# Semaphore increments without a waiter between the depthwise-convolution matmuls of a four-layer image network

## The chip, the core and the metric

The kernel runs on one core of one Trainium2 chip. The core has five engines with an instruction stream each: TensorE (matmuls; "PE" in the profile, its weight loads "PEld"), VectorE ("DVE"), ScalarE ("ACT"), GpSimd ("POOL") and SyncE ("SP", which here issues transfers). [...] an instruction may wait until a counter has a value, and may add one to a counter when it is done. The metric is the device time of one launch in microseconds.

## What is computed

The input `x` is 4 images of 48 channels, 256 by 256, in fp32. Four layers follow each other, each `x = x + layer(group_norm(x))`. Layers 1 and 2 are scans over rows and columns with a small convolution per step, and layer 0 resembles layer 3. The change is in layer 3:

```
def _L3_conv_ref(x, w_in, w_dw, fft_mask, w_out):
    ...
    y = jnp.einsum('oc,bchw->bohw', w_in, x)
    ...
    f = jnp.fft.rfft2(yp) * fft_mask[None]
    yp = jnp.fft.irfft2(f, s=(P, P))
    ...
    y = lax.conv_general_dilated(y, w_dw, window_strides=(1, 1), padding=((1, 1), (1, 1)), dimension_numbers=('NCHW', 'OIHW', 'NCHW'), feature_group_count=C2)
    x1, x2 = jnp.split(y, 2, axis=1)
    g = jax.nn.gelu(x1, approximate=False) * x2
    return jnp.einsum('oc,bchw->bohw', w_out, g)
```

48 channels are widened to 288, each 8 by 8 patch goes through a Fourier transform, is scaled and comes back, then every channel is convolved by itself with a 3 by 3 filter (the nine "taps"), the halves are gated, and 144 channels are narrowed to 48 again.

## The kernel before

Two images are worked on at once, in strips of 8 rows: 32 full strips and one tail strip of a single row for each pair of images, so 64 full strips and 2 tails in `layer3` (line 881 on). The transforms are matmuls too: `turned` (`pt`, L1006), `waves` (`pf`, L1021), `spectrum` and `spectrum_rest` (`pz`, L1040 and L1053), `pixels` and `pixels_rest` (`pp`, L1087 and L1106). They leave the strip's widened channels in SBUF tiles named `z_a0`, `z_a1` (two halves of the first 128 channels of one image), `z_b0`, `z_b1` (the other image) and `z_m` (what remains of both).

The 3 by 3 convolution is shared between two engines. VectorE computes the upper four rows of the `z_b` tiles by multiply-and-add (`begin`, L1183). Everything else goes to TensorE as matmuls with diagonal weights: a tap is the strip, shifted by the tap's offset, times a 32x32 diagonal matrix of filter values, added up in PSUM over nine taps. The array of 128x128 is used as 16 places of 32x32, four blocks of 32 channels by four groups of output partitions.

This work is cut into two "lanes". Lane 0 has channel blocks 0 and 1, lane 1 has blocks 2 and 3. A unit is one lane's nine taps for one tile: `taps` (L1117 to L1127; matmul at L1123) for `a0`, `a1` and `m`, and `lower_taps` (L1130 to L1144; matmul at L1139) for the lower rows of both `b` tiles. In both, a tap is eight matmuls of 32x512: in `taps` the row pair `j` runs from 0 to 3 and for each the two blocks of the lane; in `lower_taps` it is two halves, two row pairs and two blocks. In a tail strip `taps` has `j = 0` only, and `lower_taps` isn't called.

`together` (L1272) runs two units side by side: one tap of lane 0, one tap of lane 1, and so on nine times, with one of VectorE's multiply-adds issued now and then between them. A strip has seven units (three for each lane, and `m`, which goes to lane 0 in even strips and lane 1 in odd ones), so two strips make seven such pairs. Layer 3 is recorded under a hand-written schedule: TensorE, VectorE and ScalarE execute in the order in which the code issues.

When a unit is done its sums leave PSUM through `curve` (gelu on ScalarE, L1160) and `gate` (product on VectorE, L1166) or `lower_gate` (L1146). Between two pairs of units TensorE does transforms or the final narrowing (`mixed`, `po`, L1205 and L1215).

## Time and profile before

| | us |
|---|---|
| timed runs, median of 3 | 13250.55 (13233.93 to 13252.02) |
| profiled execution | 13259.28 |
| its span | 13257.5 |
| of it, reading the input and its statistics (0 to 230) | 230 |
| layer 0 (230 to 2790) | 2560 |
| layers 1 and 2, the scans (2790 to 8690) | 5900 |
| layer 3 (8690 to 13257) | 4567 |

The profile comes from one profiled execution. Its page gives each engine's busy time, the span in 40 slices, the DMA queues (one of them, "instruction", brings the engines' programs), the chain of work that ended last, and the costliest groups of instructions. A group is named by line, engine and operation, then the output and input tiles, the shape and a count. "Idle before" is how long the engine stood idle just ahead of that group, and behind the arrow stands what ended that wait; "issue" means that nothing that the profile shows was waited for. Semaphore instructions are not counted as busy. The ends of matmuls are modelled, and matmuls in different places of the array overlap, so a group's busy time is less than count times mean. The granted clock of TensorE over the whole execution was 0.966 of full speed.

### The profile page before, as it was taken

Reading aid. Unit: us, or ns where it says so; the run is one execution under the profiler, and the core shown is the slowest. Engines: PE = TensorE matmul, PEld = TensorE weight load, DVE = VectorE, ACT = ScalarE, POOL = GpSimd, SP = SyncE. Lnnn points to the kernel's source line nnn. Section 1 sums busy time; section 2 is a strip of 40 time slices with the busy share of each in tenths; the row PEclk is TensorE's granted clock in tenths of the full one; section 3 lists DMA queues with packets and bytes.
Section 4 is the critical chain, followed back from the end, with each engine's and each line's share of the span. In section 5 each row is a group of like instructions: output and inputs, shape, how many; then the busy total and the mean of one; then the engine's idle time right before and its main releaser. Section 6 shows DMA issues by size and latency. Waiting matters only on the chain.

```text
span 13257.5 us, 432328 instructions
## 1 busy us (share of the span) xinstructions
PE 12356.8 (93%) x203336; PEld 8155.9 (62%) x203336; DVE 7417.3 (56%) x10766; ACT 3602.9 (27%) x4043; POOL 1336.7 (10%) x977
## 2 busy tenths in 40 slices
PE   2999999998999899999998999989999999999999
PEld 1333333335777677767776777666666666666666
DVE  6777777773333334653333336556666666666666
ACT  1444444442223100002232000033333333333333
POOL 0011011010000002530000015400000000000000
PEclk9999999998999999999999999889999999999999
DMA  7222222225755876987657769711111111111110
GB/s 171 59 55 57 55 57 59 52 54 101 153 134 153 172 153 147 229 177 152 136 153 165 157 135 220 179 31 27 23 27 27 24 27 23 27 27 23 27 27 20
DMA packets 1170374, 1225.00 MB, mean 92 GB/s; under 512 B 1027669, under 2 KB 1031757, under 8 KB 1107725
## 3 DMA queue, kind: packets, MB, share of 16 engines
q1 hardware_dynamic: 1070476, 649.55, 25.6%
q0 software_dynamic: 87488, 445.55, 11.6%
q10 hardware_dynamic: 10624, 102.24, 4.4%
q8 instruction: 1592, 26.08, 0.9%
q14 instruction: 194, 1.58, 0.0%
HBM read 699.76 MB, written 497.42 MB: 90 GB/s over the span
## 4 chain that ended last, share of the span: by engine, by line
PE 88%; ACT 4%; issue 3%; DVE 3%; DMA 2%; SPq 0%; POOL 0%; DVEq 0%; ACTq 0%; POOLq 0%
PE acc L661 40%; PE pd L1123 12%; PE pd L308 9%; PE pd L1139 5%; PE pz L1040 4%; PE pp L1087 4%; PE po L1215 2%; PE ph L285 2%; PE pz L1053 2%; DMA gx<-in_x 1%; PE ph L277 1%; PE py L382 1%; PE po L452 1%; PE py L389 1%; PE po L1205 1%
## 5 line engine op out<-in xcount | busy, mean ns | idle before, releaser
L661 PE MATMUL acc<-line,w_down 96*96 96x256 f32 x12240 | 2692.9, 382 | 53.0 <-ACT line L731 31.8
L661 PEld LDWEIGHTS acc<-line,w_down 96*96 96x96 f32 x12240 | 2008.1, 164 | 730.1 <-DVE line L740 34.1
L1123 PE MATMUL pd<-z_a,diag 32*32 32x512 f32 x37152 | 1626.2, 599 | 57.8 <-issue 49.4
L308 PE MATMUL pd<-main,diag 32*32 32x512 f32 x36864 | 1427.2, 621 | 81.4 <-issue 77.3
L661 PE MATMUL acc<-line,w_right 96*96 96x256 f32 x6120 | 1341.0, 380 | 81.8 <-DVE line L811 59.8
L661 PE MATMUL acc<-line,w_left 96*96 96x256 f32 x6120 | 1362.9, 384 | 31.2 <-DVE line L852 31.2
L1183 DVE SCALAR_TENSOR_TENSOR acc<-z_b,wd,acc 128x1024 f32<-128x1024 f32 (+1 forms) x1056 | 1326.5, 1259 | 34.4 <-ACT acc L1178 7.1
L345 DVE SCALAR_TENSOR_TENSOR acc<-rest,wd,acc 128x1024 f32<-128x1024 f32 x1024 | 1257.8, 1292 | 126.9 <-ACT acc L339 126.6
L1123 PEld LDWEIGHTS pd<-z_a,diag 32*32 32x32 f32 x37152 | 890.6, 103 | 604.0 <-issue 232.9
L661 PEld LDWEIGHTS acc<-line,w_right 96*96 96x96 f32 x6120 | 1000.1, 164 | 412.6 <-DVE line L811 61.1
L661 PEld LDWEIGHTS acc<-line,w_left 96*96 96x96 f32 x6120 | 1007.9, 165 | 377.5 <-DVE line L852 47.1
L308 PEld LDWEIGHTS pd<-main,diag 32*32 32x32 f32 x36864 | 505.2, 105 | 798.1 <-issue 684.4
L1139 PE MATMUL pd<-z_b,diag 32*32 32x512 f32 x18432 | 973.7, 642 | 0.5 <-ACT z_b L999 0.5
L740 DVE TENSOR_TENSOR line<-acc,in 96x256 f32<-96x256 f32 x1020 | 428.9, 421 | 961.6 <-PE acc L661 948.7
L814 DVE SCALAR_TENSOR_TENSOR line<-acc,b_right,in 96x256 f32<-96x256 f32 x1020 | 489.4, 480 | 836.4 <-PE acc L661 836.4
L775 DVE SCALAR_TENSOR_TENSOR line<-acc,b_down,in 96x256 f32<-96x256 f32 x992 | 475.9, 480 | 811.5 <-PE acc L661 810.6
L120 ACT ACTIVATE nrm<-nrm 96x2 f32<-96x2 f32 (+2 forms) x5 | 1.0, 204 | 2989.4 <-DVE nrm L119 2989.4
L852 DVE SCALAR_TENSOR_TENSOR line<-acc,b_left,in 96x256 f32<-96x256 f32 x992 | 475.8, 480 | 564.2 <-PE acc L661 564.2
L862 POOL TENSOR_TENSOR blk<-blk,line 96x1024 f32<-96x1024 f32 x248 | 705.2, 2873 | 644.3 <-DVE line L852 644.3
L1043 DVE TENSOR_TENSOR z<-pz,mask 128x1024 f32<-128x1024 f32 x512 | 601.2, 1219 | 276.2 <-PE pz L1040 273.7
L782 ACT COPY blk<-line 96x1024 f32<-96x1024 f32 (+2 forms) x264 | 480.0, 1891 | 978.0 <-DVE line L775 816.0
L1087 PEld LDWEIGHTS pp<-c_inv,z 64*64 64x64 f32 x32768 | 515.9, 135 | 228.8 <-issue 204.6
(167 smaller groups left out, 13065.8 us busy)
## 6 DMA issues: line engine op xcount, KB each, us to landing
blk<-x ACTq DMA_DIRECT2D x64, 1536.0 KB, 19.3
in<-x SPq DMA_DIRECT2D x248, 384.0 KB, 11.0
dn<-line POOLq DMA_DIRECT2D x124, 768.0 KB, 9.6
rt<-line POOLq DMA_DIRECT2D x124, 768.0 KB, 9.6
in<-rt SPq DMA_DIRECT2D x124, 768.0 KB, 12.6
in<-dn SPq DMA_DIRECT2D x120, 768.0 KB, 5.8
in<-up SPq DMA_DIRECT2D x240, 384.0 KB, 9.3
up<-blk POOLq DMA_DIRECT2D x56, 1536.0 KB, 14.3
```

The lines of the kernel that those rows point to most:

```text
L308: nc.tensor.matmul(pd[32 * j : 32 * j + 32, i], diag[s, t, :], z[s, R2 * j + t // 3 : R2 * j + t // 3 + R2, t % 3 : t % 3 + W], start=(t = ...
L345: nc.vector.scalar_tensor_tensor(to, at(t, r), wd[:, 1, t : t + 1], to, ALU.mult, ALU.add)
L661: self.nc.tensor.matmul(acc, w[:, t, :], carry[:, :, t : t + m], start=(t == 0), stop=(t == 2))
L782: nc.scalar.copy(blk[:, :, e, lo:hi, k // 2 : k // 2 + RH], inner(ln[:, e::2])[..., lo:hi].rearrange("p h i w -> p i w h"),)
L814: nc.vector.scalar_tensor_tensor(blocks(inner(line)), blocks(acc), br, new, ALU.add, ALU.add)
L862: (nc.vector if w0 == 0 else nc.gpsimd).tensor_tensor(part, part, inner(ln[:, f::2])[..., lo:hi].rearrange("p w i h -> p i h w"), ALU.add)
L1040: nc.tensor.matmul(pz[:, b, q, :], xf[s, q0 + q, :], wi[s, NM * k : NM * k + NM], start=True, stop=True)
L1043: nc.vector.tensor_tensor(zs[k][:, q0 : q0 + 4].rearrange("p q b c -> p b q c"), pz, mask[:, :, :, NM * k : NM * k + NM].to_broadcast([128 ...
L1087: nc.tensor.matmul(pp[64 * c : 64 * c + 64, l, q, :], z[f, q0 + q, b, 64 * c : 64 * c + 64], self.inv1[f, :], start=True, stop=True,)
L1123: nc.tensor.matmul(pd[32 * j : 32 * j + 32, i, 0:n, :], diag[s, 2 if g == "m" else half, t, :], zt[g][s, R2 * j + t // 3 : R2 * j + t // 3 ...
L1139: nc.tensor.matmul(pd[to, i], diag[s, half, t, :], zt[f"b{half}"][s, R2 * j + t // 3 : R2 * j + t // 3 + R2, t % 3 : t % 3 + W], start=(t ...
L1183: nc.vector.scalar_tensor_tensor(acc, at(t), wd[:, half, t : t + 1], acc, ALU.mult, ALU.add)
```

## The change

A semaphore `pace` is allocated once, and in both tap functions an instruction that adds one to it is put into TensorE's stream: in `taps` behind every odd row pair `j`, in `lower_taps` behind each half. Either way it stands behind four matmuls of one lane. No instruction waits for `pace`, and nothing else differs.

```
+            pace = tc.alloc_semaphore("pace")
+
             def taps(step, g, half, blocks, pd):
                 for t in range(9):
                     for j in range(1 if tail(step) else 4):
...
                                 zt[g][s, R2 * j + t // 3 : R2 * j + t // 3 + n, t % 3 : t % 3 + W],
                                 start=(t == 0), stop=(t == 8),
                             )
+                        if j % 2:
+                            nc.tensor.sem_inc(pace)
                     yield True
 
             def lower_taps(step, blocks, pd):
...
                                     zt[f"b{half}"][s, R2 * j + t // 3 : R2 * j + t // 3 + R2, t % 3 : t % 3 + W],
                                     start=(t == 0), stop=(t == 8),
                                 )
+                        nc.tensor.sem_inc(pace)
                     yield True
```

In the built program each of these is one instruction of its own on TensorE, of the kind that the profile calls EVENT_SEMAPHORE.

More of the change, by code (lines that the diff above doesn't have):

```diff
@@ L1113, in pixels_rest @@
                         nc.scalar.copy(to[:, j, l], pp[64 * j : 64 * j + 64, l].rearrange("p q (h w) -> p q h w", w=8))
+            pace = tc.alloc_semaphore("pace")
             def taps(step, g, half, blocks, pd):
@@ L1127, in taps @@
                             )
+                        if j % 2:
+                            nc.tensor.sem_inc(pace)
                     yield True
@@ L1143, in lower_taps @@
                                 )
+                        nc.tensor.sem_inc(pace)
                     yield True
```

## The prediction

> **What bounds the kernel now.** I read the first lines of the page, then the chain of waits, then layer 3's stage alone, then one pair of tap units in the timeline.

> ```profile
> span 13257.5 us, 432328 instructions
> PE 12356.8 (93%) x203336; PEld 8155.9 (62%) x203336; DVE 7417.3 (56%) x10766; ACT 3602.9 (27%) x4043; POOL 1336.7 (10%) x977
> PE 88%; ACT 4%; issue 3%; DVE 3%; DMA 2%; SPq 0%; POOL 0%; DVEq 0%; ACTq 0%; POOLq 0%
> ...
> PE acc L661 40%; PE pd L1123 12%; PE pd L308 9%; PE pd L1139 5%; PE pz L1040 4%; PE pp L1087 4%; PE po L1215 2%; PE ph L285 2%; PE pz L1053 2%; DMA gx<-in_x 1%; PE ph L277 1%; PE py L382 1%; PE po L452 1%; PE py L389 1%; PE po L1205 1%
> q8 instruction: 1592, 26.08, 0.9%
> ```

> TensorE carries 88% of the chain, and the lines that the change touches carry 12% + 5% of it: 17% of 13257.5 us, 2254 us. Whatever the change adds to TensorE there lengthens the run; nothing else stands in front of it.

> ```profile
> 8690.00:13257.00 4567.00, 4376.90 (x127017) 3056.65 (x127014) 2934.61 (x3068) 1589.31 (x2325) 5.69 (x15) 0.97 0.12 25
> ```

> This is layer 3 alone (TensorE's matmuls, its loads, VectorE, ScalarE, GpSimd; then the granted clock): TensorE is busy for 4377 of 4567 us and VectorE for 2935, so no other engine is near. What TensorE waits for there is, by the view of waits, "issue" for 163.7 us (the six such rows added, 167 stalls) and everything else for 20 us.

> Now the taps themselves. Two views of one pair of units, both lanes on `z_a`:

> ```profile
> 11042.34 0.56 PEld L1123 LDWEIGHTS pd<-z_a,diag 32*32 32x32 f32 x33
> 11042.35 9.75 PE L1123 MATMUL pd<-z_a,diag 32*32 32x512 f32 x288
> ...
> 11043.23 0.55 PEld L1123 LDWEIGHTS pd<-z_a,diag 32*32 32x32 f32 x32 [0.33 <-issue]
> ...
> 11044.09 7.09 PEld L1123 LDWEIGHTS pd<-z_a,diag 32*32 32x32 f32 x223 [0.31 <-issue]
> ...
> 11051.80 1.94 ACT L1160 ACTIVATE gl<-pd 128x1024 f32<-128x1024 f32 x2 [7.24 <-PE pd L1123]
> 11052.02 1.96 PEld L1087 LDWEIGHTS pp<-c_inv,z 64*64 64x64 f32 x128 [0.84 <-issue]
> ```

> And from a neighbouring pair, the times at which one lane's eight matmuls of a tap (the first of the two records of each) begin:

> ```profile
> 11007.65 0.73 PE L1139 MATMUL pd<-z_b,diag 32*32 32x512 f32 x8
> ...
> 11008.71 0.73 PE L1139 MATMUL pd<-z_b,diag 32*32 32x512 f32 x8
> ...
> 11009.77 0.73 PE L1139 MATMUL pd<-z_b,diag 32*32 32x512 f32 x8
> ```

> A pair of units is 9 taps x 2 lanes x 8 matmuls = 144 fp32 matmuls. The trace records each as two loads and two matmuls, hence x288. One tap fills all 16 places of 32x32 in the array and takes 1.06 us. Yet a place's own work is shorter: in the first tap its second matmul begins 0.45 us after its first, later ones 0.43 us, so two take 0.86 us. The missing 0.2 us is in the loads. 33 of them run in one go: the 32 of tap one and exactly one of tap two. Then none is issued for 0.33 us. With their matmuls these are about 64 instructions, so I read it as a window of 64: a load enters when the instruction 64 places earlier has ended. A matmul's record lasts 0.587 us, so tap after tap costs 0.43 + 0.587 + some 0.03 us to notice it: 1.04 to 1.05, against 1.06 seen. The stream therefore stands still for most of a tap, since inside the bursts a whole fp32 matmul, four instructions, follows the last by 17 ns: 16 x 17 = 0.27 us of feeding per 1.06 us.

> [...] The kernel before has 199 such instructions in the same lines, all of them waits:

> ```profile
> L1123 PEldq EVENT_SEMAPHORE  x199: 51/51/827, 8688.7 to 13244.7; - x199
> ```

> So 51 ns is the floor of the price. One at 11042.367, between the lanes' first taps, is followed by the next load at 11042.443: 76 ns with what comes after. I take 51 to 76 ns.

> **The change part by part.** It removes and moves nothing: on every engine the matmuls and other operations keep their order, and only increments are put in between on TensorE. Nothing waits for the semaphore, so no other engine gets a wait. In full-size units each lane issues two increments per tap: 2 x 9 = 18 per unit, 36 per pair. There are 64 full strips with 7 lane-units each (two lanes' a0, a1 and b, one m): 448 x 18 = 8064, in 224 pairs. Tail strips have no j = 1 and no lower taps, so none. At 51 ns all of them are 411 us, if nothing hid them.

> What hides them: a tap needs 0.27 us to feed and now 4 x 51 to 76 ns more, 0.47 to 0.57 us, out of 1.06 us set by the window. Behind a waiting increment stand only the next four matmuls of the same stream. The tap keeps its length. What is not hidden is the stagger: the burst that restarts the array is fed in order, and the last four matmuls of a tap now stand behind three increments. They begin, and at the pair's end finish, 3 x 51 to 3 x 76 = 0.15 to 0.23 us later than now. This does not add up from tap to tap, since every place is bound to its own previous matmul, but it is paid once per pair: the next matmuls (`pp`, 64x64, at 11052.02) start when the last tap is out, 0.84 us after the last load. 224 x 0.15 to 0.23 = 34 to 51 us; I take 45.

> The second term is the program itself. 1592 packets of the instruction queue against 2 x 203336 recorded loads and matmuls plus 896 semaphore instructions is 256 TensorE instructions per packet. 8064 more are 31.5 packets, where layer 3 now fetches 2 x 127017 / 256 = 992. Bounds: in proportion to the 163.7 us of "issue", 5 us; one more stall of the mean length (163.7 / 167 = 0.98 us) for each packet, 31 us. [...] I take 25. It can also fall below nothing: packet borders land at other instructions, and a border that stalls now may fall inside a tap.

> Sum: 45 + 25 = 70 us on the profiled execution's 13259.3 us. The median of the timed runs is 8.7 us below that execution, so 13250.6 + 70, about 13320 us, 0.5% slower.

> **The rivals.**
> - An increment takes a place in the window. Then 64 places hold 60 loads and matmuls, a load of the next tap waits for one fp32 matmul more and the increment before it: 17 + 51 = 0.07 us per tap, 0.6 us per pair, with the stagger 0.78 us. 224 x 0.78 = 175 us, with fetching 13450 us. [...] Against: the increment at 11042.367 ran while most of lane 0's loads of that tap were still to come, so it is done ahead of them and need not stay.
> - Nothing hides them: each increment stops the stream for its 51 ns or lets what is before it run out. 411 us and fetching: 13690 us. Against it: semaphore instructions in the trace run ahead of matmuls that precede them.
> - Faster: spacing the stream. Every four matmuls now start some 50 to 76 ns apart instead of 17, so the loads of the next tap meet places that ended at different times, and the 0.2 us of a tap in which the array waits for its window shrinks. All of it is 224 x 8 x 0.2 = 358 us; half, with fetching against it, gives about 13095 us. It decides if the tap falls from 1.06 towards 0.86 us. For it: the loss is one of order and timing, not of work, and the first places of the second tap do run back to back. Against: three in four matmuls still follow each other at 17 ns.
> - No change that can be measured: stagger hidden by the next stage's own start, and borders that fall well: 13250 us.

> **How the numbers follow.** A measurement of this kernel tells about 0.2%, 26 us, from no change. Chances: forecast 0.45, a place in the window 0.15, nothing hidden 0.05, faster by spacing 0.22, no change 0.13. So slower 0.65, same 0.13, faster 0.22. The forecast's own range is 34 + 5 to 51 + 31 with the borders' luck, 13280 to 13350 us. The range that should hold 8 in 10 takes in no change, the window case up to 13480 and the mild end of the faster case from 13150; it leaves out the unhidden case and most of the spacing gain.

> **What would show it.** Right: the line of semaphore instructions in TensorE's stream grows by 8064 at 51 ns, taps stay 1.06 us apart, the pair grows from 9.75 to about 9.9 to 10.0 us, the instruction queue shows some 1624 packets, and "issue" in layer 3 rises from 164 us by a few tens. Window rival: taps at 1.13 us. Unhidden: over 1.2 us. Spacing: taps under 1.0 us and a pair under 9.3 us. A shift of the clock's 0.97 in layer 3 would be a part that I have not priced. The forecast is wrong if the taps' distance changes at all.

## The result, and the profile after

| | before | after |
|---|---|---|
| median of the runs | 13242.24 us | 14688.42 us |
| lowest to highest | 13214.9 to 13252.02 us | 14638.6 to 14697.02 us |
| ratio, 95% interval | 1 | 1.1088 [1.1057, 1.1119] |
| span of the profiled execution | 13257.5 us | 14691.8 us |
| layer 3 (from 8690 us of the span on) | 4567 us | 6001 us |

The changed kernel is 11% slower: 1446 us, where 70 had been forecast. It lies in layer 3: the first tap there starts at 8690.3 us before and at 8683.9 after. The first lines of the page of the kernel after (engines; the chain that ended last; the queue that brings instructions):

```profile
span 14691.8 us, 440392 instructions
PE 12941.8 (88%) x203336; PEld 8683.8 (59%) x203336; DVE 7425.0 (51%) x10766; ACT 3603.5 (25%) x4043; POOL 1333.9 (9%) x977
PE 84%; issue 8%; ACT 3%; DVE 2%; DMA 2%; SPq 0%; POOL 0%; DVEq 0%; ACTq 0%; POOLq 0%
...
q8 instruction: 1623, 26.59, 0.8%
```

The instructions grew by 8064 exactly. The instruction queue moved 31 packets more, where 31.5 had been worked out. But "issue", time in which TensorE waits for nothing that the profile shows, grew from 3% to 8% of the chain. Layer 3 alone, in the view by windows (matmuls, loads, VectorE, ScalarE, GpSimd, then the granted clock):

```profile
8690.00:14691.00 6001.00, 4947.69 (x126842) 3579.81 (x126833) 2935.75 (x3063) 1587.16 (x2322) 5.68 (x15) 0.93 0.09 19
```

Of 1434 us more, TensorE is busy for 571 (4377 to 4948) and idle for 863. VectorE's and ScalarE's work is unchanged. The clock went from 0.97 to 0.93. The waits of TensorE in layer 3, first before, then after (total us, times, longest; the matmuls of L1123 and L1139 stand at L1125 and L1143 in the kernel after):

```profile
PE pf L1021 <- issue: 58.5, 42, 2.7
PE pd L1123 <- issue: 49.6, 46, 2.3
PE pp L1087 <- issue: 49.3, 67, 1.9
```

```profile
PE pd L1125 <- issue: 516.5, 270, 4.2
PE pp L1087 <- issue: 276.6, 188, 2.5
PE pd L1143 <- issue: 147.2, 79, 2.6
PE pf L1021 <- issue: 61.0, 42, 2.6
PE pz L1040 <- issue: 18.2, 20, 2.1
```

"issue" rose from 163.7 us in 167 stalls to 1025.7 us in 605: that is 862 of the 863 us of idle time. The rows that grew are the taps themselves (`pd`) and the transform that follows them (`pp`); `pf`, which has no taps right ahead of it, stayed. One pair of units in the timeline of the kernel after, loads and matmuls (start, length; in brackets the idle time ahead):

```profile
12002.41 0.71 PEld L1125 LDWEIGHTS pd<-z_a,diag 32*32 32x32 f32 x33 [2.38 <-issue]
12002.44 4.68 PE L1125 MATMUL pd<-z_a,diag 32*32 32x512 f32 x120 [1.50 <-issue]
12003.29 2.91 PEld L1125 LDWEIGHTS pd<-z_a,diag 32*32 32x32 f32 x87 [0.18 <-issue]
...
12009.04 0.67 PEld L1125 LDWEIGHTS pd<-z_a,diag 32*32 32x32 f32 x33 [2.84 <-issue]
12009.04 3.95 PE L1125 MATMUL pd<-z_a,diag 32*32 32x512 f32 x64 [1.93 <-issue]
```

Between two stalls lie 33 + 87 loads, 120 matmuls and 16 increments: 256 instructions, one packet of the instruction queue. The stalls end 6.63 us apart, and after 3.8 us of loads nothing is there to be issued for 2.84 us. The same holds all over: counted in the records, 582 of 635 gaps of over 0.8 us between two starts in layer 3's stream sit at the same place of the count modulo 256, the border of a packet (123 of 135 before). So I read these gaps as TensorE waiting for its program, not for its array. Added up, the gaps of over 0.15 us at these borders are 244 us before and 1307 after: 1063 of the 1434 us. Each increment itself is as small as expected:

```profile
L1148 PEldq EVENT_SEMAPHORE  x2304: 51/51/51, 8732.3 to 14655.3; - x192
```

From the records I also took the length of one packet, from border to border, where both borders show a stall (so that fetching sets it), against the increments in it: 3.48 us with none (these are packets of the transforms), 4.30 with four, 5.27 with eight, 6.90 with fifteen. That is 0.23 us for each, while the packet's own taps take some 4.1 us whatever their number. So a packet with no increment comes in 3.5 us, less than the 4.24 us of its taps (256 / 64 x 1.06), and one with fifteen takes longer than they do.

The trace also has the transfers of the instruction queue, and they show where this time goes. In the view of DMA queues, first a packet of taps of the kernel before (11044.70 to 11048.90 us), then the packet of the timeline above (12002.33 to 12009.04, its first increment included). Each window reaches from one border to the next and is cut into 40 slices; the digit stands where the one transfer in it begins:

```profile
DMA  0000000007000000000000000000000000000000
q8 instruction: 1, 0.02, 2.0%
```

```profile
DMA  0000000000000000000000000300000000000000
q8 instruction: 1, 0.02, 0.8%
```

The packet that is fetched while this one runs starts on its way 1.05 us behind the border in the first, and 4.28 us behind it in the second. The packets of the kernel after with stalls at both borders divide in this way (medians):

| increments in the packet | border to the start of the next transfer, us | the transfer, us | its end to the next border, us |
|---|---|---|---|
| none (49 packets) | 1.13 | 1.05 | 1.37 |
| fifteen (134 packets) | 4.40 | 1.06 | 1.35 |

So the increments lengthen neither the transfer nor what follows it. They delay its start, and in 274 of the 312 packets of taps all of the packet's increments had gone before it. The question for the runs: what about an increment delays the fetching.

### The profile page after: what moved, and what is told of

Its sections match the earlier page's. It is cut to its first block, busy times and chain, and to the rows that moved or that the text cites. A ratio compares the mean times of both kernels' runs of the same rounds, so it can differ in the third digit from the quotient of the medians.

```text
span 14691.8 us, 440392 instructions
## 1 busy us (share of the span) xinstructions
PE 12941.8 (88%) x203336; PEld 8683.8 (59%) x203336; DVE 7425.0 (51%) x10766; ACT 3603.5 (25%) x4043; POOL 1333.9 (9%) x977
## 4 chain that ended last, share of the span: by engine, by line
PE 84%; issue 8%; ACT 3%; DVE 2%; DMA 2%; SPq 0%; POOL 0%; DVEq 0%; ACTq 0%; POOLq 0%
PE acc L661 36%; PE pd L1125 13%; PE pd L308 8%; PE pd L1143 5%; PE pp L1087 4%; PE pz L1040 4%; PE po L1220 2%; PE pz L1053 2%; PE ph L285 2%; PE ph L277 1%; DMA gx<-in_x 1%; PE py L382 1%; PE po L452 1%; PE po L1210 1%; PE py L389 1%
## 5 line engine op out<-in xcount | busy, mean ns | idle before, releaser
L661 PE MATMUL acc<-line,w_down 96*96 96x256 f32 x12240 | 2693.1, 382 | 52.5 <-ACT line L731 31.2
L661 PEld LDWEIGHTS acc<-line,w_down 96*96 96x96 f32 x12240 | 2008.5, 164 | 729.4 <-DVE line L740 34.1
L1125 PE MATMUL pd<-z_a,diag 32*32 32x512 f32 x37152 | 1938.1, 638 | 441.1 <-issue 434.1
L1125 PEld LDWEIGHTS pd<-z_a,diag 32*32 32x32 f32 x37152 | 1040.0, 106 | 937.8 <-issue 731.3
L308 PE MATMUL pd<-main,diag 32*32 32x512 f32 x36864 | 1434.0, 625 | 76.0 <-issue 72.4
L661 PE MATMUL acc<-line,w_right 96*96 96x256 f32 x6120 | 1341.0, 380 | 81.7 <-DVE line L811 59.9
L661 PE MATMUL acc<-line,w_left 96*96 96x256 f32 x6120 | 1362.8, 384 | 31.2 <-DVE line L852 31.2
L661 PEld LDWEIGHTS acc<-line,w_right 96*96 96x96 f32 x6120 | 1000.2, 164 | 412.4 <-DVE line L811 61.2
L1143 PE MATMUL pd<-z_b,diag 32*32 32x512 f32 x18432 | 1108.8, 658 | 147.8 <-issue 147.2
L661 PEld LDWEIGHTS acc<-line,w_left 96*96 96x96 f32 x6120 | 1007.9, 165 | 377.5 <-DVE line L852 47.1
L308 PEld LDWEIGHTS pd<-main,diag 32*32 32x32 f32 x36864 | 503.8, 105 | 796.9 <-issue 680.9
L1087 PE MATMUL pp<-c_inv,z 64*64 64x64 f32 x32768 | 664.8, 238 | 283.3 <-issue 278.0
L1087 PEld LDWEIGHTS pp<-c_inv,z 64*64 64x64 f32 x32768 | 605.5, 152 | 498.6 <-issue 475.7
L1125 PE MATMUL pd<-z_m,diag 32*32 32x512 f32 x9288 | 710.1, 616 | 82.3 <-issue 82.3
```

The source lines that it names most:

```text
L308: nc.tensor.matmul(pd[32 * j : 32 * j + 32, i], diag[s, t, :], z[s, R2 * j + t // 3 : R2 * j + t // 3 + R2, t % 3 : t % 3 + W], start=(t = ...
L661: self.nc.tensor.matmul(acc, w[:, t, :], carry[:, :, t : t + m], start=(t == 0), stop=(t == 2))
L1087: nc.tensor.matmul(pp[64 * c : 64 * c + 64, l, q, :], z[f, q0 + q, b, 64 * c : 64 * c + 64], self.inv1[f, :], start=True, stop=True,)
L1125: nc.tensor.matmul(pd[32 * j : 32 * j + 32, i, 0:n, :], diag[s, 2 if g == "m" else half, t, :], zt[g][s, R2 * j + t // 3 : R2 * j + t // 3 ...
L1143: nc.tensor.matmul(pd[to, i], diag[s, half, t, :], zt[f"b{half}"][s, R2 * j + t // 3 : R2 * j + t // 3 + R2, t % 3 : t % 3 + W], start=(t ...
```

## The experiments

All are edits of the kernel after unless said otherwise. "issue" and the clock are those of layer 3, a "pair" is the median time from the first to the last start of the matmuls of a pair of units, taken from the records (9.57 us before, 14.30 after). "Next transfer" is the median time from the border to the start of the next packet's transfer, over the packets of layer 3 that hold nothing but taps; "border gaps" adds up the gaps of over 0.15 us at all of layer 3's borders.

| run | increments | ratio, 95% interval | "issue" us (stalls) | pair us | clock | next transfer us | border gaps us |
|---|---|---|---|---|---|---|---|
| before | 0 | 1 | 164 (167) | 9.57 | 0.97 | 1.01 | 244 |
| e2_every24 | 1344 | 1.0044 [1.0028, 1.0061] | 188 (185) | 9.44 | 0.97 | 0.99 | 271 |
| e1_every8 | 4032 | 1.0194 [1.0179, 1.0209] | 319 (310) | 9.66 | 0.97 | 1.29 | 447 |
| after | 8064 | 1.1088 [1.1057, 1.1119] | 1026 (605) | 14.30 | 0.93 | 4.38 | 1307 |
| e10_six | 12096 | 1.0768 [1.0741, 1.0794] | 684 (617) | 12.99 | 0.97 | 3.27 | 963 |
| e3_every2 | 16128 | 1.0782 [1.0761, 1.0804] | 371 (397) | 13.46 | 0.97 | 3.04 | 633 |
| e11_every | 32256 | 1.2112 [1.2089, 1.2135] | 132 (132) | 22.18 | 0.98 | 2.47 | 177 |
| e9_two, two in a row | 8064 | 1.0291 [1.0268, 1.0315] | 373 (362) | 10.88 | 0.97 | 1.72 | 535 |
| e12_four, four in a row | 8064 | 1.0178 [1.0161, 1.0195] | 281 (270) | 9.77 | 0.97 | 1.43 | 410 |
| e7_bunch, 18 in a row | 8064 | 1.1087 [1.1071, 1.1104] | 1090 (298) | 9.36 | 0.85 | 0.89 | 144 |
| e4_nop | 8064 no-operations | 1.0359 [1.0344, 1.0375] | 414 (500) | 11.07 | 0.97 | 2.28 | 658 |
| e8_wait | 8064 waits | 1.0004 [0.9994, 1.0015] | 164 (159) | 9.47 | 0.97 | 1.04 | 243 |

**How dense: e1_every8, e2_every24, e3_every2.**

```
-                        if j % 2:                   (taps)
-                        nc.tensor.sem_inc(pace)     (lower_taps)
+ e1_every8:             if j == 3: ...  /  if half == 1: ...
+ e2_every24:            if j == 3 and t % 3 == 2: ...  /  if half == 1 and t % 3 == 2: ...
+ e3_every2:             if not tail(step): ...  /  the same increment inside the loop over j
```

> An increment behind every eighth matmul: 4032 instead of 8064. Theory 'fetch' (each increment holds up the fetching of TensorE's next 256-instruction packet by 0.23 us, and it costs nothing while the fetch is still quicker than the work): a packet of taps now takes 3.5 + 7.7 x 0.23 = 5.3 us to fetch against 4.2 us of work, 2.3 packets per pair, some of it made up between the pairs; +300 to +650 us over before, less than half of the change. Rival 'toll' (each increment stops the stream for its own 0.18 us): half of the change, +720 us. Rival 'no fetching ahead' (a packet that holds any increment has its successor fetched only when it is used up): nearly all of the change, above +1100 us.

> An increment behind every twenty-fourth matmul of a lane: 1344. Theory 'fetch': a packet of taps takes 3.5 + 2.5 x 0.23 = 4.1 us to fetch against 4.2 us of work, so next to nothing is left over: 0 to +120 us over before. Rival 'toll': 1344 x 0.18 = +240 us. Rival 'no fetching ahead': above +800 us.

> An increment behind every second matmul: 16128. Theory 'fetch': a packet of taps takes 3.5 + 28 x 0.23 = 10 us to fetch, 2.5 packets per pair, 25 us per pair against 9.8 us before: 224 x 15 = +3400 us over before, a little less where it is made up between pairs; +3000 to +3600. Rival 'toll': 16128 x 0.18 = +2900 us.

Half of after's increments cost 253 us over before's median, a sixth 47, so up to four per tap the cost rises faster than the number. (The 253 us lie below all three ranges that were expected of e1_every8, the 47 us in that of its fetch theory.) With twice after's number the cost fell, to 1026 us, where 2900 and more had been expected, and "issue" went back to 371 us:

```profile
PE pp L1087 <- issue: 203.9, 205, 1.9
PE pd L1125 <- issue: 83.0, 105, 2.8
```

What is slow in e3_every2 is the program's arrival only in part: the gaps at borders, 633 us, are 389 over before's, of some 975 us more in layer 3. The view by windows has TensorE busy for 5142 of 5542 us, and its increments mostly stand 151 ns apart, with eight loads and matmuls between them: 8 x 0.151 = 1.21 us per tap at the least, over the 1.06 us that a tap took before. So an increment costs the sequencer (the part of TensorE whose records the views mark `PEldq`) 0.151 us, not the 0.051 of its record; and a fixed price on fetching for each increment can't be, since sixteen thousand of them have less "issue" than eight thousand, and their next transfer begins earlier (3.04 us against 4.38).

**Is it the semaphore? e4_nop and e8_wait.**

```
e4_nop:   -nc.tensor.sem_inc(pace)   +nc.tensor.nop(hint="pace", nofuse=True)
e8_wait:  -nc.tensor.sem_inc(pace)   +nc.tensor.wait_ge(pace, 1)      (the value is there from the start)
```

> In each increment's place a no-operation that the sequencer runs and that touches no semaphore. If it is the sequencer's time that holds up the fetching: about as slow as the change, +1000 to +1500 us over before, with stalls at packet borders. If it is the semaphore's update: +30 to +110 us (8064 instructions more to fetch and feed), no more. If program length alone did it: the same as the change, but then a filler of matmuls of the same number would too.

> In place of each of the 8064 increments stands a wait on the same semaphore for a value that it has from the start; the compiler hangs these waits onto the matmuls themselves, so the stream gets no instruction of its own (some 1592 packets as before). Theory 'own instruction' (the harm is that a stand-alone instruction has to pass the sequencer in order): within 0.3% of before, 13240 +- 40 us, 'issue' in layer 3 160 to 200 us. Rival 'semaphore' (any use of a semaphore between the matmuls holds the stream or its fetching): 13400 to 14700 us, with 'issue' over 300 us.

In e8_wait the compiler hung nearly all of the waits onto matmuls: TensorE's stream has 322 instructions more than before, not 8064. Layer 3 is what it was before:

```profile
8690.00:13246.40 4556.40, 4363.95 (x126724) 3060.15 (x126718) 2926.72 (x3061) 1582.81 (x2322) 5.68 (x15) 0.97 0.12 25
```

In e4_nop the instruction stayed and the semaphore went. It costs a third of after's (3.6%, 470 us, between the two ranges that were expected) and has 414 us of "issue". Its record and its distance in a row differ as an increment's do, 13 ns and 90 ns:

```profile
L1148 PEldq NOP  x2304: 13/13/13, 8703.0 to 13652.3; - x192
```

So no semaphore is needed for the harm: instructions of their own between the matmuls do it without one. The no-operation does less of it than the increment. It also occupies the sequencer for less time (90 ns in a row against 151), but whether that or the missing update makes the difference isn't separated; nor was an increment tried that a matmul carries.

**Is it the larger program? e5_filler** (an edit of the kernel before, no increments):

```
+            def filler(step, blocks, pd, z):
+                for j in range(0 if tail(step) else 4):
+                    nc.tensor.matmul(
+                        pd[32 * j : 32 * j + 32, 0, 0:1, 0:1], diag[32 * blocks[0] : 32 * blocks[0] + 32, 0, 0, :],
+                        z[32 * blocks[0] : 32 * blocks[0] + 32, 0:1, 0:1],
+                        start=True, stop=True,
+                    )
...
+                filler(step, blocks, pd, zt[g])          (ahead of the nine taps; zt["b0"] in lower_taps)
```

> No increments; four more fp32 matmuls of one column ahead of each unit's first tap, whose results the first tap overwrites: 1792 matmuls, each four instructions in the stream, 7168 instructions more against 8064 in the change. Theory 'fetch by increments': the packets grow as in the change (some 1620), but the time by 224 x 8 x 0.017 = 30 us plus up to 30 us, +20 to +100 us over before. Rival 'length' (the longer program alone): above +1000 us.

28 packets more (1620), 1.0046 [1.0029, 1.0062], 57 us for the matmuls and their packets together; "issue" 155 us, no more than before. The 57 us also hold the 1792 matmuls, which had been expected at 30 us. So some 30 packets more do little harm as packets, and the prediction's reading of them can't account for the loss.

**Somewhere else: e6_layer0** (an edit of the kernel before: increments in layer 0's taps in the same rhythm, none in layer 3).

```
+                                if j % 2:
+                                    nc.tensor.sem_inc(pace)      (behind layer 0's matmul, L308 of before)
```

> The same increments behind every fourth matmul of a lane, but in layer 0's taps and none in layer 3's: 4608. Layer 0 uses up a packet in 7.1 us (2 x 46194 / 256 = 361 packets in 2560 us), and with 12.8 increments fetching one takes 3.5 + 2.9 = 6.4 us. Theory 'fetch': mostly hidden, +50 to +400 us over before. Rival 'toll': 4608 x 0.18 = +830 us.

1.0211 [1.0189, 1.0233]: 273 us over its before (13518.48 against 13245.25) for 4608 increments, 0.06 us each against after's 1446 / 8064 = 0.18. "issue" rose there as well. The first 3000 us, before and then e6_layer0:

```profile
PE pd L308 <- issue: 77.3, 43, 3.1
```

```profile
PE pd L310 <- issue: 126.1, 55, 6.2
```

By its last matmuls layer 0 ends at 3055 us before, not at 2790 as in the table of stages, and at 3315 us in e6_layer0; to there the second line would read 137.5 us. The next transfer begins 1.03 us behind the border before and 2.46 in e6_layer0 (medians of the packets that are mostly taps), so the effect isn't one of layer 3's code. A packet of layer 0's taps lasts 7.1 us before, over the 4.1 of layer 3's, which leaves more room for a late one; that this is why less of it shows is my reading. "issue" took 91 us of the 260 that layer 0 grew by, and the rest stands in TensorE's busy time, which this run doesn't divide further.

**Where they stand: e7_bunch, e9_two, e12_four.** The number is after's 8064 in all three.

```
e9_two:    behind a lane's tap:         if j == 3: two sem_inc in a row     (lower_taps: if half: the same)
e12_four:  behind a tap of lane 1:      if blocks[0]: four in a row, none in lane 0
e7_bunch:  behind a unit's ninth tap:   for _ in range(18): nc.tensor.sem_inc(pace)
```

> The same 8064 increments, but a unit's 18 all together behind its last tap. Program length is that of the change. Theory 'fetch' with a fixed hold-up per increment wherever it stands: the sum of the fetching is the same, so the time is within 25% of the change, +1050 to +1800 us over before. If spread increments do the harm by touching every packet: per pair 36 x 0.076 = 2.7 us in a row, partly beside the last tap's drain, 224 x 1.5 to 2.7 = +340 to +600 us.

> The same 8064 increments, but two in a row behind the last matmul of each lane's tap, in place of one behind every fourth. Theory 'held at the head' (an increment waits at the sequencer until the matmuls ahead of it are handed over, and meanwhile the next packet is not asked for; the second of a row waits no more): the number of such places is that of the kernel with one per eight matmuls (1.019), so 1.02 to 1.06, 'issue' 320 to 600 us. Rival 'per increment' (each increment lengthens a packet's fetching by some 0.25 us wherever it stands): as after, 1.10 to 1.115, 'issue' near 1000 us.

> The same 8064 increments again, four in a row behind each tap of lane 1, none in lane 0: one place per tap, where after has four and the kernel with two in a row has two. 'Held at the head' (each place holds the sequencer's fetching some 0.28 us, and the further increments of the row add only their 0.151 us of the sequencer's own time, which the tap's 1.06 us covers: 0.27 + 0.60 us): 'issue' in layer 3 165 to 260 us, ratio 1.005 to 1.03, the last part from the row's 0.45 us standing between the lanes, at up to 1.3 us per pair. 'Per increment': as after, 1.10 or more, 'issue' near 1000 us.

With the same 8064 increments the time follows the number of places where they interrupt a tap, up to these four: four places 1.109, two 1.029, one 1.018. Two in a row per lane's tap cost 1.029 where one there cost 1.019 (e1_every8): twice the number at the same places adds one per cent, and the same number at twice the places (after) eight more. e9_two's time and "issue" and e12_four's time are in the forecast ranges; e12_four's "issue" of 281 us is a little over its 165 to 260. e12_four's undisturbed pairs (no gap of over 0.5 us) take 9.17 us at the median against 9.16 before, so 4 x 0.151 us in one piece are hidden beside a tap.

e7_bunch is a different case and lands at after's time, and in the range of its fetch theory, by coincidence. Its taps are undisturbed (9.36 us per pair), but both units of a pair end together, and 36 increments pass one by one ahead of the next matmuls. First its longest row in the view of waits, then one such place in the timeline, then the increments of that place (the view of one source line, from 11995 to 12002 us):

```profile
PE pp L1087 <- issue: 851.4, 192, 4.8
```

```profile
12001.86 3.24 PEld L1087 LDWEIGHTS pp<-c_inv,z 64*64 64x64 f32 x128 [5.35 <-issue]
12001.89 3.35 PE L1087 MATMUL pp<-c_inv,z 64*64 64x64 f32 x128 [4.47 <-issue]
```

```profile
L1133 PEldq EVENT_SEMAPHORE  x36: 51/51/51, 11996.4 to 12001.8; - x36
```

36 in 5.4 us is 0.151 each, again at 51 ns recorded, and no load passes in 5.35 us. The `pp` behind it then runs slower: 3.24 us for its 128 loads, where the one shown before took 1.96. The granted clock from 12001.86 to 12005.20 us is 0.57. In layer 3 of this run TensorE has the half clock for 1759 us against 314 before.

**Over a tap's own pace: e10_six and e11_every.**

```
e10_six:    if j: sem_inc        (lower_taps: if half or j == 3)     six per tap
e11_every:  sem_inc behind each matmul of a full strip               sixteen per tap
```

> Six increments per tap (three per lane), 12096 in all, between after's four and the eight of the kernel with one behind every second matmul. At 0.151 us each a tap needs 0.27 + 6 x 0.151 = 1.18 us to feed, just over the 1.06 us of the window. 'Held at the head': matmuls rarely wait for the window, so fetching gets on and the time lies below after's: 1.04 to 1.08, 'issue' 300 to 600 us, taps 1.15 to 1.2 us apart. 'Per increment': over after, 1.13 to 1.20, 'issue' over 1200 us.

> An increment behind every matmul of the taps, 32256 in all. If an increment costs the sequencer 0.151 us, as their distance in a row was, and matmuls are fed beside it: taps 16 x 0.151 = 2.4 us (or 2.7 us, if the feeding adds to it) apart; a pair grows from 9.6 to some 22 to 24 us, 224 x 12 to 14.5 = 2700 to 3250 us more: ratio 1.20 to 1.25, 'issue' about as before plus what the profile counts between matmuls. 'Per increment' on fetching: 51 increments in a packet at 0.25 us on top of 3.5 us make 16 us per packet of 3.2 taps, 5 us per tap: 1.6 or more. At the 51 ns of the record alone: 16 x 0.051 + 0.27 = 1.09 us per tap, 1.01 to 1.03.

Half as many increments again as after has, and 3.2% less of before's time: "issue" fell from 1026 to 684 us. (684 is over the 600 that I gave it, and the median distance of taps, 1.09 us, under the 1.15 to 1.2.) At every matmul it is gone:

```profile
PE 15177.0 (95%) x203336; PEld 11022.4 (69%) x203336; DVE 7425.6 (46%) x10766; ACT 3610.6 (23%) x4043; POOL 1332.3 (8%) x977
```

```profile
8690.00:16033.40 7343.40, 7183.00 (x127019) 5923.11 (x127016) 2942.72 (x3068) 1595.92 (x2325) 5.69 (x15) 0.98 0.08 16
```

A pair takes 22.18 us, 2.46 per tap, where 16 x 0.151 = 2.42: the sequencer's time for the increments sets the pace, and the matmuls are fed beside it. A packet with 51 increments lasts 8.04 us (51 x 0.151 = 7.7), and fetching the next fits in; what is left of "issue" is less than before's.

**What the runs show together.** Two costs were separated. One is the sequencer's 0.151 us per increment. It costs nothing while a tap has room for it (e12_four's four per tap: 0.27 + 0.60 us of 1.06), and is the whole cost at sixteen. The other is lateness of the next packet, and it is largest at four single increments per tap. From the start of its transfer a packet needs 1.05 + 1.37 = 2.42 us, and these two parts are nearly the same in all runs of the table (medians of 0.99 to 1.13 us over the packets of taps, and of 1.38 to 1.41 us where a stall of over 0.8 us follows). By an estimate from these numbers a packet of taps lasts as long as its own work or until the next one's transfer has begun and 2.42 us more are over, whichever is longer. For after that sum is 6.80 us, for e10_six 5.69, e3_every2 5.46, e4_nop 4.70, and the medians of these packets are 6.87, 5.70, 5.42 and 4.72 us. For e12_four it is 3.85 us, which fits into the 4.1 us of the taps, and for e11_every 4.89 us of 8.04. (Single packets scatter around these medians: e9_two's sum is 4.14, and some of its packets are late.)

Why the start of the transfer is delayed is less sure. My reading, an estimate from the 4.40 us of packets with fifteen increments against the 1.13 of those with none, is that an increment that comes up while the prediction's window of 64 is full waits at the head of the stream, and that the next packet's transfer isn't started while it waits. The window is itself an estimate, from the 33 loads that run in one go. e9_two, e10_six and e12_four were forecast from this, and their times came out ("issue" did only in e9_two); in terms of the packets' lengths what goes beyond 3.48 us, divided by the increments of the packet, is 0.23 us in after, 0.15 in e9_two (0.29 for its two together), 0.10 in e10_six and 0.08 in e3_every2. It stays a reading: the trace has the transfers but nothing that shows what sets off their start, and no run showed the window itself. What is shown is that at one number of increments the time depends on where they stand, that instructions of their own do the harm without a semaphore, and that most of the loss appears at packet borders because the next transfer begins late.

The clock's share isn't isolated by any run. In the records of layer 3 the half clock is granted for 902 us after against 314 before; by an estimate that takes all of that difference as matmuls at half speed, 588 / 2 = 294 us of the 1434 are its part at most. Gaps of 2.2 us and more in the stream went from 14 to 309. Of the 209 half-clock stretches after, 136 have such a gap in the 8 us ahead of them (3 of 65 before), and begin at the median 0.48 us behind its end; these gaps are themselves 2.7 us long at the median. The other 73 stretches have none. Of the 209 stretches 173 last 3.41 us each. That the gaps bring the half clock about was not shown. TensorE's busy time grew for another reason too, since a pause of the stream is partly hidden under the last matmuls: in the timeline above the loads stood still for 2.84 us where the matmuls show 1.93.

No kernel here is faster than the one before.

## Why the prediction was wrong

The forecast was 13320 us in a range of 13150 to 13480. It had the sign and missed the size twentyfold, 70 us against 1446. By its steps:

- *TensorE is the bound of layer 3, and what is added to its stream lengthens the run*: held. No other engine's work changed, and TensorE's waits for other engines in layer 3 stayed small (20 us before, 23 after).
- *A tap takes 1.06 us because of a window of 64, and is fed in 0.27 us of it*: the length held where no packet is late; the window stays an estimate from the 33 loads in one go, and no run showed it. In the records the median distance of taps is 1.04 us before and 1.07 after; four increments in one piece (e12_four) left undisturbed pairs at 9.17 us; eight and sixteen per tap moved that median to 1.33 and 2.50 us.
- *51 to 76 ns per increment*: wrong. 51 ns is the record; the distance in a row is 151 ns (e7_bunch, e11_every). The 76 ns were the distance from a wait of the kernel before to the next load, not from one increment to another. At 4 x 0.151 us the cover of 1.06 us still sufficed, so this error alone didn't upset the sum.
- *The stagger term, 45 us*: right in kind, small in size. Pairs without a stall grew from 9.16 us to 9.47 for the shortest and 9.73 at the median of the six that there are (no gap of over 0.5 us): 0.3 to 0.6 us where 0.15 to 0.23 were worked out, at most 224 x 0.57 = 128 us in place of 45.
- *The fetch term, 25 us*: this is the step that failed. Its count was right (31.5 packets forecast, 31 seen). Its mechanism was that 31 packets more are 31 chances more of a stall, with bounds of 5 and 31 us; e5_filler shows that packets alone are indeed cheap. But the increments made the packets that were there before arrive late: the next transfer begins 4.38 us behind the border in place of 1.01, the gaps at packet borders grew by 1063 us, and "issue" in layer 3 by 862. The sum took the 1.06 us of a tap as cover for the feeding, the increments and the fetching alike, and asked only if the array would still be fed. That an increment could delay the fetching was in none of the terms.
- *The clock of layer 3, named as not priced*: fell from 0.97 to 0.93; at most 294 us.
- *The rival in which nothing hides them, 411 us from 8064 x 51 ns, taken as the worst case*: it wasn't the worst. It counts the increments' own time alone, and most of the loss came from packets whose transfer began late.

The rival of a place in the window asked for taps 1.13 us apart and the one of wider spacing for less than 1.0; at a median of 1.07 neither is there. The trace of the kernel before held a hint: in layer 3's packets of taps the next transfer begins 1.01 us behind the border of the packet that is being executed, so its start could be delayed by what that packet holds. Most borders in layer 3 were crossed without a stall before (167 stalls for some 992 packets), and far fewer after (605 stalls for some 1024).

## What to carry to other kernels

An instruction that only the sequencer executes isn't free because nobody waits for it: take its price from the distance of two in a row, not from its record, and look at whether the stretch lives close to the arrival of its program: stalls marked "issue" at every 256 instructions, and transfers of the instruction queue that begin late behind such a border. In a stretch of many small matmuls put such instructions together at one place where the array has work in hand, or hang them onto an instruction that is there anyway (shown for waits alone): 8064 waits, nearly all hung onto matmuls, cost nothing measurable, 8064 increments cost 1.8% in rows of four and 10.9% one by one. A row must still be shorter than the work that covers it, or it stands in front of the next matmuls: with 18 in a row per unit no load passed for 5.35 us at the pair's end shown, the granted clock of layer 3 was 0.85 instead of 0.97, and the kernel was 10.9% slower.
